# Two projected map tiles and four accumulator tiles for the preparation of keys and values, in place of one and three

## Chip, cores and metric

The kernel runs on one core of one Trainium2 chip. The metric is the device time of one execution in microseconds (us); lower is better. The times before are the median, lowest and highest of three runs.

## What is computed

The input x is 8 images of 256 channels by 32 x 32 positions. Layer 0 normalises each image in groups, projects it to keys and values (kv_w), pools each projected map to four sizes (32, 16, 11 and 5 on a side, together 1426 positions), adds to each a 3 x 3 depthwise convolution, normalises over the channels, and lets 1024 queries in 8 heads attend to the 1426 keys. Layer 1 is a second attention over 1024 tokens and a gated sum of 8 expert networks. All data are float32. The part that the change touches is this:

```python
kv = jnp.einsum('bchw,oc->bohw', x, kv_w)
k_map, v_map = (kv[:, :C], kv[:, C:])
def pooled(t):
    outs = []
    for i, r in enumerate(POOL_RATIOS):
        ...
        p = jnp.einsum('bchw,ph,qw->bcpq', t, Mh, Mw)
        p = p + _depthwise(p, dconv_w[i], dconv_b[i])
        outs.append(p.reshape(B, C, -1))
    return jnp.concatenate(outs, axis=2)
ks_ = _layernorm(pooled(k_map).transpose(0, 2, 1), norm_w, norm_b)
vs_ = _layernorm(pooled(v_map).transpose(0, 2, 1), norm_w, norm_b)
```

## The kernel before, in words

Layer 0's attention (function `attention`) is a main loop over 8 batches x 2 halves of the heads x 2 halves of the queries x 12 chunks of keys, 384 steps in all. A step multiplies queries by keys into the only score tile `sc`[...], ACT takes the exponential into one of six probability tiles `pt`, and PE multiplies the probabilities of the step before by the values into `pv`. Since there is one score tile, the scores of a step wait for the exponential of the step before. Every second step GpSimd issues a DMA that adds one probability tile to another (`add`), and DVE adds these pairs up over the 12 chunks (`sums`).

Between the steps everything else is laid in: preparation of later batches and layer 1 of earlier ones. Who comes next is decided when the program is built, by the class `Flow`: it carries an estimate of each engine's clock, of when each tile is ready and of when its reader is done. Work comes in generators ("threads") with a rank; each says with `yield pe(...)`, `yield ve(...)` and so on what it needs next, or with `yield until(...)` which condition. `step` resumes the lowest-ranked thread that can run, within credits of PE time for each step (`PACE` 4 for ranks under 5, `PACE1` 2 for the others). `finish` lays in work until a condition holds, for example at the beginning of each third of a batch's keys.[...]

The preparation of a batch b is two chains:

- `prepare(b)`, rank 4, one batch after the other: load the image into `xi` (one tile), statistics, normalise, `pool_levels` (pooled input of the three small sizes into `xl`, one tile; GpSimd and DVE), then `maps`, then `queries`, which project the queries and store them to DRAM. The projections are linear, so the pooled input is projected instead of the projected map being pooled.
- `convolve`, rank 7: the taps of each finished map, 8 for each of the four sizes, all on DVE. Then `keys_and_values`, rank 2: `value_tokens` and `key_tokens` transpose the maps, normalise them over the channels and put the keys back.

`maps` takes the four maps of a batch in the order 2, 3 (values), 0, 1 (keys). Each has three slices of columns: two of 512 (the largest size) and one of 402 (the three small sizes). ACT copies each slice from PSUM into the projected map `p`, and writes the middle tap with the bias into the accumulator `acc`. The lists `todo` and `done` hold projected maps and those whose taps are all issued; `read` counts the maps whose taps of the largest size are issued; `freed` counts half batches (two maps) whose accumulators have been turned into tokens. Before the change there is one tile `pmap` for p, and three tiles for `acc`. A map's first two slices wait until all earlier maps' largest taps are issued, and its third slice until all earlier maps are done.

For batch 0 `first_maps` and `first_taps` do the same in another order, with the taps of the large key maps as matmuls on PE; there the third accumulator tile serves as p of map 3. `todo` is given four empty entries for it and `done` gets its four accumulators at the end of `first_taps`.

The last part, the experts, follows attention with its own tiles. A second, general path behind a test (`layer0_general`) is not executed with this data; the diff changes a tile count in it. `kernel` builds the program[...].

Of the kernel before, what the change touches and what calls it, by code (L numbers as in the profile page):

```python
# [142 lines left out]
def layer0_general(tc, kit, nb, x, t1, consts, consts8, vecs, q_t, kv_t, proj_t, gqk_t):  # L143
    nc = tc.nc
    T = kit.tile
    with ExitStack() as ctx:
# [106 lines left out]
        def prepare_keys(b):  # L253

            xt = xs[b]
            st = T(work, [P, 2, 2, 6], "st")
            mv = T(work, [P, 2, 2], "mv")
            for k in range(2):
                for h in range(2):
                    nc.vector.bn_stats(st[:, k, h, :], xt[:, k, h * 512 : (h + 1) * 512])  # L260
                nc.vector.bn_aggr(mv[:, k, :], st[:, k, :, :].rearrange("p h s -> p (h s)"))
            mean, var = mv[:, :, 0], mv[:, :, 1]
            yield
            gm = T(psum, [P, 512], "sm")
            nc.tensor.matmul(gm[:, 0:2], lhsT=grp, rhs=mean, start=True, stop=True)
            mu = T(work, [P, 2], "mu")
            nc.vector.tensor_copy(mu, gm[:, 0:2])
            dev = T(work, [P, 2], "dev")
            nc.vector.tensor_tensor(dev, mean, mu, ALU.subtract)
            nc.vector.tensor_tensor(dev, dev, dev, ALU.mult)  # L270
            nc.vector.tensor_tensor(dev, dev, var, ALU.add)
            yield
            yield
            gv = T(psum, [P, 512], "sm")
            nc.tensor.matmul(gv[:, 0:2], lhsT=grp, rhs=dev, start=True, stop=True)
            gr = T(work, [P, 2], "gr")
            kit.rstd(gr, gv[:, 0:2], 1e-5)
            yield
            xp = xps[b] = T(work, [P, 2, NK], "xp", bufs=2)
            for k in range(2):  # L280
                nc.vector.tensor_scalar(
                    xp[:, k, 0:HW], xt[:, k, :], mu[:, k : k + 1], gr[:, k : k + 1], ALU.subtract, ALU.mult
                )
            yield
            img = xp[:, :, 0:HW].rearrange("p k (h w) -> p k h w", h=32)

            def level(s):
                n = SIDES[s]
                return xp[:, :, OFFS[s] : OFFS[s] + n * n].rearrange("p k (h w) -> p k h w", h=n)


            t2 = T(work, [P, 2, 32, 16], "pool")
            nc.gpsimd.tensor_tensor(t2, img[:, :, :, 0::2], img[:, :, :, 1::2], ALU.add)
            nc.gpsimd.tensor_tensor(level(1), t2[:, :, 0::2, :], t2[:, :, 1::2, :], ALU.add)
            flat = xp[:, :, OFFS[1] : OFFS[2]]
            nc.gpsimd.tensor_scalar(flat, flat, 0.25, 1.0, ALU.mult, ALU.mult)
            yield

            t3 = T(work, [P, 2, 32, 11], "pool")
            nc.gpsimd.tensor_tensor(t3, img[:, :, :, 0::3], img[:, :, :, 1::3], ALU.add)  # L300
            nc.gpsimd.tensor_tensor(t3[:, :, :, 0:10], t3[:, :, :, 0:10], img[:, :, :, 2::3], ALU.add)
            nc.gpsimd.tensor_tensor(t3[:, :, :, 1:11], t3[:, :, :, 1:11], img[:, :, :, 2::3], ALU.add)
            l3 = level(2)
            nc.gpsimd.tensor_tensor(l3, t3[:, :, 0::3, :], t3[:, :, 1::3, :], ALU.add)
            nc.gpsimd.tensor_tensor(l3[:, :, 0:10, :], l3[:, :, 0:10, :], t3[:, :, 2::3, :], ALU.add)
            nc.gpsimd.tensor_tensor(l3[:, :, 1:11, :], l3[:, :, 1:11, :], t3[:, :, 2::3, :], ALU.add)
            flat = xp[:, :, OFFS[2] : OFFS[3]]
            nc.gpsimd.tensor_tensor(
                flat, flat, con[:, None, K_S11 : K_S11 + 121].to_broadcast([P, 2, 121]), ALU.mult
            )  # L310
            yield

            t5 = T(work, [P, 2, 32, 5], "pool5")
            ends = [(i * 32 // 5, -(-(i + 1) * 32 // 5)) for i in range(5)]
            for i, (a, e) in enumerate(ends):
                nc.vector.tensor_reduce(t5[:, :, :, i], img[:, :, :, a:e], AX.X, ALU.add)
            l5 = level(3)
            for i, (a, e) in enumerate(ends):
                nc.vector.tensor_reduce(
                    l5[:, :, i, :], t5[:, :, a:e, :].rearrange("p k h w -> p k w h"), AX.X, ALU.add  # L320
                )
            flat = xp[:, :, OFFS[3] : NK]
            nc.vector.tensor_tensor(flat, flat, con[:, None, K_S5 : K_S5 + 25].to_broadcast([P, 2, 25]), ALU.mult)
            yield
            acc = ks[b] = T(work, [P, 2, NK], "acc", bufs=3)
            for m in range(2):
                yield from project_and_convolve(b, m, acc)
            yield from kit.layernorm(acc, acc, NK, 1e-5, work, psum, (vec[:, V_NW:], vec[:, V_NB:]))

        def prepare_values(b):  # L330
            acc = vs[b] = T(work, [P, 2, NK], "acc", bufs=3)
            for m in range(2):
                yield from project_and_convolve(b, 2 + m, acc)
            yield from kit.layernorm(acc, acc, NK, 1e-5, work, psum, (vec[:, V_NW:], vec[:, V_NB:]))
# [560 lines left out]
def attention(tc, kit, f, outer, ended, nb, consts, x, t1, t2, hn, bounds, vecs, q_t, kv_t, proj_t, gqk_t, wqk, wqkv, vecs1, w1_d, w1c, gate_d, wrc, vecs2, bnvec):  # L895
# [6 lines left out]
    with ExitStack() as ctx:  # L902
# [5 lines left out]
        def T(pool, shape, tag, bufs=1):  # L908
            return f.tile(pool, shape, tag, bufs=bufs)
# [154 lines left out]
        ks, qs, vts = {}, {}, {}  # L1064
        made = [0]
        turn = [-1]
        todo, done, read, freed, key_parts, normalised = [], [], [4], [0], [0], [0]

        def pe(*tiles, tag=None):
            return "PE", tiles, tag  # L1070
# [10 lines left out]
        def until(cond):  # L1081
            return None, cond, None
# [5 lines left out]
        def maps(xp):  # L1088

            for m in (2, 3, 0, 1):  # L1090
                c = m % 2
                yield until(lambda: read[0] >= len(todo) and len(todo) < 3 + 2 * freed[0])
                p = pmap
                acc = T(work, [P, NK], "acc", bufs=3)
                for s0, w in KEY_SLICES:
                    if s0 >= HW:
                        yield until(lambda: len(done) >= len(todo))
                    src = source(xp, s0, w)
                    yield pe(src, tag="sm")
                    ps = small()  # L1100
                    for k in range(2):
                        f.pe.matmul(
                            ps[:, :w],
                            lhsT=kvw[:, k, m * P : (m + 1) * P],
                            rhs=src[:, k, :],
                            start=k == 0,
                            stop=k == 1,
                        )
                    f.act.activation(p[:, s0 : s0 + w], ps[:, :w], AF.Copy)
                    for s, n in enumerate(SIDES):  # L1110
                        a, z = max(OFFS[s], s0), min(OFFS[s] + n * n, s0 + w)
                        if a < z:
                            f.act.activation(
                                acc[:, a:z],
                                ps[:, a - s0 : z - s0],
                                AF.Identity,
                                bias=db(c, s),
                                scale=mid[:, c * 4 + s : c * 4 + s + 1],
                            )
                todo.append((c, p, acc))  # L1120
# [4 lines left out]
            return dy, dx, max(0, -dy), n - max(0, dy), max(0, -dx), n - max(0, dx)  # L1125


        pmap = T(work, [P, NK], "p")
        f.split(pmap, 512, HW)
        first, large, whole, pooled, asked = {}, [], [], [], []  # L1130

        def first_diagonals():
# [11 lines left out]
        def first_maps(xp):  # L1144


            for m in range(4):
                if m < 2:
                    p = T(work, [P, 4, 512], "pt", bufs=6).rearrange("p j q -> p (j q)")
                    acc = T(l1, [P, NK], "v") if m else T(work, [P, NK], "kn", bufs=3)  # L1150
                else:
                    p = T(work, [P, NK], "acc", bufs=3) if m == 3 else pmap
                    acc = T(work, [P, NK], "acc", bufs=3)
                for t in (p, acc):
                    if t is not pmap:
                        f.split(t, 512, HW)
                first[m] = p, acc
            for m, s0 in [(m, s0) for g in (0, 2) for s0 in (0, 512) for m in (g, g + 1)] + [(m, HW) for m in range(4)]:
# [70 lines left out]
        def first_taps():  # L1229
            for m in (2, 3):  # L1230
                yield until(lambda: "maps" in large)
                yield from taps(m - 2, 0, *first[m])
                large.append(("values", m))
            yield until(lambda: whole)
            for m in (2, 3, 0, 1):
                for s in range(1, 4):
                    yield from taps(m % 2, s, *first[m])
                whole.append(m)
            done.extend(first[m][1] for m in (2, 3, 0, 1))
# [1310 lines left out]
```

## Time and profile before

| | |
|---|---|
| three runs, median (lowest to highest) | 3303.81 us (3302.39 to 3315.54) |
| profiled execution, time and span | 3310.0 us, 3308.1 us |
| mean granted clock of TensorE | 0.979 |
| PE, DVE, ACT, POOL busy | 3098.8, 2455.2, 1733.4, 1217.1 us |
| first and last score matmuls of layer 0 | 80.3 and 1953.8 us |
| taps on the accumulators | 928 from p, 32 from an accumulator tile; median 445 ns |
| adds of probabilities by GpSimd's DMAs | 160 of 1024 KB, 32 of 144 KB |

The profile is of one execution. A row of the timeline gives start, length, engine, line of the helper that issued it (all 669 here, so one goes by tile names), operation, output<-inputs and, in brackets, the idle time before it with what ended it. A row of a stretch gives its bounds and length, then busy us and instructions of PE, PEld (weight loads), DVE, ACT and POOL, then the granted clock, the busy share of the DMA engines and GB/s. In the strip of 40 slices each digit is a tenth.

### The profile page before, as it was taken

Reading aid. Unit: us, or ns where it says so; the run is one execution under the profiler, and the core shown is the slowest. Engines: PE = TensorE matmul, PEld = TensorE weight load, DVE = VectorE, ACT = ScalarE, POOL = GpSimd, SP = SyncE. Lnnn points to the kernel's source line nnn. Section 1 sums busy time; section 2 is a strip of 40 time slices with the busy share of each in tenths; the row PEclk is TensorE's granted clock in tenths of the full one; section 3 lists DMA queues with packets and bytes.
Section 4 is the critical chain, followed back from the end, with each engine's and each line's share of the span. In section 5 each row is a group of like instructions: output and inputs, shape, how many; then the busy total and the mean of one; then the engine's idle time right before and its main releaser. Section 6 shows DMA issues by size and latency. Waiting matters only on the chain. (4 is left out here: it accounts for less than half of the span.)

```text
span 3308.1 us, 57168 instructions
## 1 busy us (share of the span) xinstructions
PE 3098.8 (94%) x23038; PEld 1790.7 (54%) x23038; DVE 2455.2 (74%) x4068; ACT 1733.4 (52%) x2330; POOL 1217.1 (37%) x1315
## 2 busy tenths in 40 slices
PE   8687899999999999999899889999999999999997
PEld 4322234334334334334334236767888888888886
DVE  5687688797886887987875455447888787777776
ACT  4476675675676576666666543343333344444442
POOL 2211411412213213213112112007656567777775
PEclk9798999999999999999999999999999999999999
DMA  2357655745646756655556557125434310000000
GB/s 75 84 127 165 131 100 145 147 93 143 142 103 143 147 132 131 132 133 114 125 127 143 122 119 246 60 86 178 153 134 153 139 65 20 20 25 27 20 14 21
DMA packets 110754, 362.70 MB, mean 110 GB/s; under 512 B 13504, under 2 KB 38856, under 8 KB 87248
## 3 DMA queue, kind: packets, MB, share of 16 engines
q0 software_dynamic: 28608, 179.85, 28.2%
q1 hardware_dynamic: 78512, 177.13, 15.5%
q8 instruction: 184, 3.01, 0.4%
q10 hardware_dynamic: 3360, 1.97, 0.2%
q14 instruction: 90, 0.74, 0.1%
HBM read 112.45 MB, written 81.31 MB: 59 GB/s over the span
## 5 line engine op out<-in xcount | busy, mean ns | idle before, releaser
L669 ACT ACTIVATE pt<-sc 128x2048 f32<-128x2048 f32 (+1 forms) x384 | 720.5, 1876 | 298.5 <-PE sc L669 246.5
L669 DVE SCALAR_TENSOR_TENSOR acc<-p,vec,acc 128x225 f32<-128x225 f32 (+7 forms) x928 | 532.7, 580 | 31.3 <-ACT acc L669 6.5
L669 PE MATMUL sc<-q,kn 32*128 32x512 f32 (+1 forms) x3072 | 448.1, 653 | 108.0 <-ACT pt L669 105.8
L669 DVE TENSOR_TENSOR pt<-pt,pt 128x1024 f32<-128x1024 f32 x320 | 384.4, 1244 | 144.3 <-DMA pt<-pt 133.1
L669 POOL DMA_DIRECT2D pt<-pt x192 | 171.4, 894 | 769.3 <-ACT pt L669 592.9
L669 PE MATMUL pv<-pt,vt 128*32 128x512 f32 (+1 forms) x3072 | 420.2, 620 | 0.0
L669 ACT ACTIVATE p1c<-bank 128x256 f32<-128x256 f32 x230 | 87.9, 382 | 565.9 <-PE bank L669 554.3
L669 ACT ACTIVATE h<-h,bnvec 128x512 f32<-128x512 f32 x460 | 348.0, 805 | 63.8 <-DVE h L669 54.7
L669 POOL TENSOR_TENSOR rstd<-rstd,mhalf 128x4 f32<-128x4 f32 (+2 forms) x88 | 108.8, 1237 | 697.7 <-DVE rstd L669 586.3
L669 DVE TENSOR_TENSOR h<-p1c,bank 128x512 f32<-128x512 f32 x230 | 156.7, 681 | 211.6 <-PE bank L669 211.0
L669 PEld LDWEIGHTS sc<-q,kn 32*128 32x128 f32 (+1 forms) x3072 | 116.8, 179 | 320.2 <-ACT pt L669 217.8
L669 POOL TENSOR_TENSOR tm<-h,tm 128x256 f32<-128x256 f32 x210 | 241.8, 1151 | 16.5
L669 DVE TENSOR_TENSOR h<-u,bank 128x256 f32<-128x256 f32 x460 | 234.3, 550 | 7.9
L669 PEld LDWEIGHTS pv<-pt,vt 128*32 128x32 f32 (+1 forms) x3072 | 60.9, 108 | 304.2 <-issue 295.1
L669 POOL TENSOR_TENSOR tm<-h 128x512 f32<-128x512 f32 x105 | 137.9, 1313 | 195.2 <-ACT h L669 194.1
L669 DVE TENSOR_TENSOR h<-h,gate 128x1024 f32<-128x1024 f32 x128 | 203.2, 1588 | 0.5 <-ACT h L669 0.5
L669 PE MATMUL bank<-h,w2e 128*128 128x256 f32 (+1 forms) x604 | 193.3, 448 | 2.8 <-DVE h L669 1.9
L669 PE MATMUL sm<-p,v 128*32 128x256 f32 (+1 forms) x2416 | 192.3, 379 | 0.7 <-ACT p L669 0.7
L669 PE MATMUL y<-t,s3e 128*128 128x256 f32 x768 | 187.0, 379 | 2.2 <-POOL t L669 2.1
L669 PE MATMUL bank<-t,s1e 128*128 128x256 f32 x750 | 183.8, 381 | 3.5 <-DVE h L669 3.5
L669 POOL TENSOR_TENSOR t<-h,t 128x256 f32<-128x256 f32 x216 | 172.9, 800 | 17.0
L669 POOL TENSOR_TENSOR t<-h 128x512 f32<-128x512 f32 x108 | 140.1, 1298 | 105.4 <-DVE h L669 80.0
(315 smaller groups left out, 5448.6 us busy)
## 6 DMA issues: line engine op xcount, KB each, us to landing
pt<-pt POOLq DMA_DIRECT2D x160, 1024.0 KB, 7.5
h<-h SPq DMA_DIRECT2D x118, 512.0 KB, 3.3
xi<-in_x_dram SPq DMA_DIRECT2D x16, 512.0 KB, 6.7
t<-t SPq DMA_DIRECT2D x8, 1024.0 KB, 5.6
res<-t SPq DMA_DIRECT2D x32, 256.0 KB, 4.7
t<-res SPq DMA_DIRECT2D x32, 256.0 KB, 4.6
hn<-res SPq DMA_DIRECT2D x32, 256.0 KB, 4.2
hn<-hn SPq DMA_DIRECT2D x16, 512.0 KB, 4.4
```

Source lines behind the costliest of these rows:

```text
L669: ins = fn(*args, **kwargs)
```

## The change

There are two tiles for p, used in turn, and four for `acc`, in the executed path and in the general one. The conditions are loosened accordingly: a map's first two slices wait until all earlier maps but one have their largest taps issued, its third slice until all earlier maps but one are done. Two maps of batch 1 may be projected before batch 0's accumulators are free; after that two maps for each half batch freed, one more than before in all. `read` begins at 2 and is raised by the two value maps of batch 0. Map 3 of batch 0 has the second tile for its p, no accumulator tile. The room comes from the descriptors of GpSimd's DMAs, which get 4096 bytes of a partition.

```diff
@@ general path: prepare_keys, prepare_values
-            acc = ks[b] = T(work, [P, 2, NK], "acc", bufs=3)
+            acc = ks[b] = T(work, [P, 2, NK], "acc", bufs=4)
...
-            acc = vs[b] = T(work, [P, 2, NK], "acc", bufs=3)
+            acc = vs[b] = T(work, [P, 2, NK], "acc", bufs=4)
@@ attention
-        todo, done, read, freed, key_parts, normalised = [], [], [4], [0], [0], [0]
+        todo, done, read, freed, key_parts, normalised = [], [], [2], [0], [0], [0]
@@ maps
-                yield until(lambda: read[0] >= len(todo) and len(todo) < 3 + 2 * freed[0])
-                p = pmap
-                acc = T(work, [P, NK], "acc", bufs=3)
+                yield until(lambda: read[0] >= len(todo) - 1 and len(todo) < (4 + 2 * max(freed[0], 2) if freed[0] else 6))
+                p = pmaps[len(todo) % 2]
+                acc = T(work, [P, NK], "acc", bufs=4)
                 for s0, w in KEY_SLICES:
                     if s0 >= HW:
-                        yield until(lambda: len(done) >= len(todo))
+                        yield until(lambda: len(done) >= len(todo) - 1)
@@ attention
-        pmap = T(work, [P, NK], "p")
-        f.split(pmap, 512, HW)
+        pmaps = [T(work, [P, NK], f"p{i}") for i in range(2)]
+        for t in pmaps:
+            f.split(t, 512, HW)
@@ first_maps
-                    p = T(work, [P, NK], "acc", bufs=3) if m == 3 else pmap
-                    acc = T(work, [P, NK], "acc", bufs=3)
+                    p = pmaps[m - 2]
+                    acc = T(work, [P, NK], "acc", bufs=4)
                 for t in (p, acc):
-                    if t is not pmap:
+                    if t is not p or m < 2:
                         f.split(t, 512, HW)
@@ first_taps
                 large.append(("values", m))
+                read[0] += 1
@@ kernel
-    nc = _bacc.Bacc("TRN2", target_bir_lowering=False, num_devices=1)
+    nc = _bacc.Bacc("TRN2", target_bir_lowering=False, num_devices=1, dynamic_dma_scratch_size=4096)
```

## The prediction

> **What bounds the kernel now.** I read first the busy shares and the strip of 40 slices on the page, then the busy time of each engine in stretches cut at the batches of the convolution layer's attention, then the same by quarter batch ("unit": one half of the heads, 512 queries, 12 score steps), then the timeline around one hand-over between two maps, and last the DMA and form rows.
>
> ```profile
> PE 3098.8 (94%) x23038; PEld 1790.7 (54%) x23038; DVE 2455.2 (74%) x4068; ACT 1733.4 (52%) x2330; POOL 1217.1 (37%) x1315
> ...
> PE   8687899999999999999899889999999999999997
> ...
> DVE  5687688797886887987875455447888787777776
> ...
> PEclk9798999999999999999999999999999999999999
> ```
>
> TensorE is busy 94%; it is idle 3308.1 - 3098.8 = 209 us. Its low digits, and the low clock, stand in slices 2 to 5 (about 80 to 410 us): the first attention batch and the start of the second. Cut by batch (PE, PEld, DVE, ACT, POOL busy, then clock):
>
> ```profile
> 80.00:325.00 245.00, 184.70 (x1393) 66.97 (x1392) 188.50 (x385) 150.49 (x175) 49.14 (x60) 0.89 0.55 122
> 325.00:562.00 237.00, 217.04 (x2090) 79.04 (x2082) 183.44 (x317) 153.91 (x183) 58.18 (x68) 0.95 0.60 130
> 562.00:811.00 249.00, 234.59 (x2276) 99.58 (x2272) 201.22 (x362) 157.39 (x195) 66.85 (x79) 0.99 0.58 127
> 1041.00:1270.00 229.00, 217.64 (x2224) 83.29 (x2220) 193.71 (x334) 152.42 (x185) 58.07 (x65) 0.99 0.63 137
> 1506.00:1746.00 240.00, 226.12 (x2368) 87.30 (x2360) 190.40 (x339) 155.21 (x191) 57.72 (x71) 0.99 0.57 121
> ```
>
> Length less the first number: PE is idle 60.3 us in batch 0, 20.0 in batch 1, 14.4, (not shown) 9.7, 11.4, (not shown) 9.9, 13.9 and 11.2 in batches 2 to 7: 151 of all 209 us. DVE is idle 35 to 57 us in each of batches 0 to 6. So attention is PE-bound from batch 2 on, with holes; in batches 0 and 1 PE lacks work. By unit:
>
> ```profile
> 325.00:382.00 57.00, 49.98 (x328) 15.68 (x324) 30.10 (x56) 37.98 (x43) 27.77 (x34) 0.86 0.67 132
> ...
> 1041.00:1108.00 67.00, 62.99 (x642) 24.69 (x638) 54.69 (x86) 41.41 (x55) 24.02 (x28) 1.00 0.59 116
> 1108.00:1154.00 46.00, 39.86 (x340) 11.62 (x332) 42.98 (x70) 27.10 (x22) 12.66 (x15) 0.96 0.72 160
> 1154.00:1214.00 60.00, 59.86 (x684) 22.84 (x680) 53.98 (x91) 46.68 (x64) 9.35 (x10) 1.00 0.52 107
> ```
>
> In a steady batch the hole is the second unit: PE idle 6.1 of 46 us while DVE is idle only 3.0; in the unit before, DVE is idle 12.3. DVE lies fallow while preparation is at its load and pooling, then is the limit when the maps' taps come. The hand-over between two maps, on ACT and on DVE:
>
> ```profile
> 1099.20 0.51 ACT L669 ACTIVATE p<-sm 128x402 f32<-128x402 f32 x1 [1.18 <-DVE acc L669]
> ```
>
> ```profile
> 1093.45 5.65 DVE L669 SCALAR_TENSOR_TENSOR acc<-p,vec,acc 128x225 f32<-128x225 f32 x17
> 1101.18 1.76 DVE L669 RECIPROCAL rec<-sx 128x256 f32<-128x256 f32 x1 [2.08 <-ACT sx L669]
> ...
> 1106.37 2.36 DVE L669 TENSOR_TENSOR pt<-pt,pt 128x1024 f32<-128x1024 f32 x2 [1.22 <-DMA pt<-pt]
> 1108.65 3.75 DVE L669 SCALAR_TENSOR_TENSOR acc<-p,vec,acc 128x961 f32<-128x961 f32 x3
> ```
>
> The third slice of the next map cannot go into the one map tile until the last tap of the map before has read it (1099.10); its taps begin at 1108.65, and DVE was idle 3.3 us in between. In the whole run ACT waited 40.3 us, 23 times, for such taps.
>
> [...] the same tap forms, first beside GpSimd's pooling (94 to 104 us), then without it (1094 to 1100 us):
>
> ```profile
> L669 DVE SCALAR_TENSOR_TENSOR acc<-acc,vec,acc 128x20 f32<-128x20 f32 x4 | 2.2, 554 | 0.1
> L669 DVE SCALAR_TENSOR_TENSOR acc<-acc,vec,acc 128x110 f32<-128x110 f32 x4 | 2.0, 490 | 0.1
> ```
>
> ```profile
> L669 DVE SCALAR_TENSOR_TENSOR acc<-p,vec,acc 128x110 f32<-128x110 f32 x4 | 1.3, 334 | 0.1
> L669 DVE SCALAR_TENSOR_TENSOR acc<-p,vec,acc 128x20 f32<-128x20 f32 x4 | 1.0, 242 | 0.1
> ```
>
> [...] the score group that takes 1.14 us took 2.09 at 385.27, and the unit 325 to 382 had clock 0.86. [...] The trace has 28608 packets for GpSimd's 220 DMAs, 130 each or 8.1 per engine[...].
>
> **The change, part by part.** No instruction is added or taken away; the work is issued in another order.
>
> *First start.* Before, the first map of batch 1 waits until batch 0's keys and values are all normalised: its slices run at 160.58 and its taps from 169.10. Its pooled input is ready at 112.3. New: the large slices of two maps may go as soon as both value maps have their large taps (62 us), so from 112 on; the small slice when all first taps end (146.7). A slice takes 1.90, 1.90 and 1.54 us on PE, so taps can start near 150, 19 us earlier, where DVE was idle 7.0 and 4.9 us. Taps of one batch are 74 us of DVE (73.8, 74.4 and 74.9 in three batches) and the four maps ran from 169 to 311, 142 us. DVE was idle 25 us of those; if half of that is recovered, they end at 150 + 142 - 13 = 279, 32 us earlier. Preparation's PE work is 4 x 5.34 (maps) + 4 x 1.90 (queries) + some 13 (48 transposes or so of 0.27) = 42 us. Of it 32/142, or 10 us, crosses from batch 1 into batch 0, into 30 us of PE holes in its last three units: **-10**. The large slices go into the first unit's wait (PE busy 69 of 99 us there), 7.6 us of PE; I count 5, since the bounds on that are 0 and 7.6: **-5**.
>
> *Batch 1.* The next preparation loads its x only after the last query projection; the load was issued at 316.7 and its maps began at 371.7. With batch 1's maps through 32 us earlier, two maps (10.7 us of PE) reach the holes of the first two units (7.0 + 7.5 us): **-8** (bounds 0 and -15).
>
> *Batches 2 to 6.* PE idles 59 us there, 31 of them in the second units. The hand-over bubble goes (3 us of DVE, four maps a batch), and load and pooling of the next batch come to lie beside taps of this one. But PE is the bound: only its holes can be won, and filling a hole earlier is a gain only if that filler is not missed later. I take a third of 31: **-10** (bounds 0 and -31).
>
> *Clock.* Units 2 and 3 of batch 0 and 0 and 1 of batch 1 lose 36 x 0.11 + 39 x 0.05 + 50 x 0.14 + 39 x 0.04 = 14.5 us to the granted clock; fuller units win about half: **-7** (0 to -14).
>
> *Costs.* Pooling (some 27 us of GpSimd a batch) moves beside taps. At 0.24 us more per small tap of 0.5, all of it covered would cost DVE 13 us a batch; DVE's 35 to 57 us of idle hide most. I put 1 us a batch on the path: **+7** (0 to +40). With preparation move 2 loads, the 1 MB copy of x (11.7 us to land), 4 query stores and 2 fetches on SP's queue; behind them stand layer 1's loads (4 to 6 us), whose users sit behind several units of other filler: 0. GpSimd's adds issued in between (0.89 us each) keep their order.
>
> *The ring.* [...] Adds are issued once in two steps (6.3 us at the quickest) and land after
>
> ```profile
> pt<-pt POOLq DMA_DIRECT2D x160, 1024.0 KB, 7.5
> ```
>
> so two are in flight. 0; were only one to fit, 1.2 us each at the quickest pace, some 160 of them less than half exposed: +60 at the very most, which I hold for unlikely. Map 3 of batch 0 now lies in the second map tile instead of an accumulator tile: same instructions, 0.
>
> Sum: -10 - 5 - 8 - 10 - 7 + 7 = -33. The profiled execution took 3310.0 us around a span of 3308.1, so 3277 for it; it lies 6.2 above the median of the runs. Against the median 3303.8 - 33 = **3271**.
>
> **Rivals.** *More than that* (3235): preparation runs ahead by most of a batch, and the two long steps that end batches 1 and 2 (21 and 23 us, keys being finished under a full stop) go too. For it: the bounds above add to -75 without them. Against it: PE was busy in those steps (72.7 of 76 us), so little is lost there. *Filler only changes places* (3298): PE does the same work in attention and what is filled early is missed in later units; only the early start is left, about 6 us. For it: 94% busy, and units 2 and 3 with PE idle 0.1 to 1.1 us. *DVE becomes the bound* (slower): with two maps ready, taps of two follow one another without pause, 37 us of taps in a unit, beside (193 - 74)/4 = 30 us of other DVE work: 67 us against units of 46 to 60. DVE runs in order, so the adds of probabilities (2.36 us a pair) stand behind taps, and the six probability tiles come free late, on which ACT's exponential and then the scores wait. It decides from 1.5 maps in a unit (27 us of taps in 57). At 10 us in one unit of six batches: +60 - 33 = +27, 3331. For it: DVE idle is already 3.0 us in second units. Against it: ACT waited for probability tiles only 24.7 us in the whole run, and DVE has 35 us a batch to spare. *It does not do what it says*: the slices find no PSUM tile or no room in the step, and the order stays; 3304, counted with the second.
>
> **Numbers.** Forecast 0.50 (own range 3250 to 3290); more 0.13; places only 0.21; DVE 0.16. About 0.5% (16.5 us) is what a measurement of this kernel can tell from no change: bounds 3287.3 and 3320.3. Faster: 0.47 + 0.13 + 0.02 = 0.62; same 0.03 + 0.19 = 0.22; slower 0.16. The range 3230 to 3325 leaves out the lower end of "more" and the upper half of "DVE".
>
> **What would show it.** First taps of batch 1 near 150 us; PE idle in the first two batches from 80 towards 55 us, clock there above 0.89 and 0.95; x loads of each batch earlier against its attention; second units with more than 40 us of PE; ACT's wait for taps under 40.3 us; the add still landing in 7.5 us. Wrong it would be if batches 2 to 6 grow, with ACT waiting for probability tiles or GpSimd's adds issuing slower than 0.9 us.

## The result

| | before | after |
|---|---|---|
| median (lowest to highest), 12 runs each on one chip | 3312.31 us (3300.66 to 3317.42) | 3311.52 us (3307.55 to 3318.98) |
| ratio of after to before, 95% interval | | 1.0004 (0.9992 to 1.0017) |
| span of the profiled execution | 3308.1 us | 3310.1 us |
| PE busy and idle in it | 3098.8 and 209.3 us | 3104.6 and 205.5 us |

The change moves the time by nothing that can be measured; 33 us less had been forecast. The page of the kernel after, its busy shares and three strips:

```profile
PE 3104.6 (94%) x22906; PEld 1793.9 (54%) x22906; DVE 2471.6 (75%) x4067; ACT 1735.5 (52%) x2329; POOL 1220.6 (37%) x1309
...
PE   8788879989999989999989889999999999999998
...
DVE  6798989898889869877545545346888887787776
...
PEclk9898989999999999999999999999999999999999
```

DVE's strip is the one that changed: 8s and 9s from slice 2 on, and the low stretch in the middle begins earlier, because the preparation is through earlier (the last tap ends at 1525 us, before at 1719). PE's digits and clock at the start are about as low as they were. Cut by batch (columns as before: length, then PE, PEld, DVE, ACT and POOL busy, then the clock):

```profile
81.00:340.00 259.00, 203.93 (x1485) 75.26 (x1487) 219.44 (x450) 159.12 (x199) 68.26 (x80) 0.89 0.53 119
340.00:575.00 235.00, 203.75 (x1824) 69.84 (x1816) 205.26 (x344) 158.42 (x194) 62.88 (x70) 0.95 0.59 125
...
1530.00:1738.00 208.00, 193.61 (x2028) 75.28 (x2025) 111.06 (x191) 137.07 (x152) 41.83 (x48) 0.99 0.65 135
1942.00:2267.00 325.00, 313.42 (x1254) 219.07 (x1247) 156.30 (x276) 112.08 (x192) 35.45 (x63) 0.97 0.37 129
```

These are batches 0, 1 and 6 and the stretch between attention and the bulk of the experts. The work has moved as foreseen: 22 us of PE work more in batch 0, and batch 6 is 32 us shorter since its preparation is done. But the stretch behind attention grew by 29 us (before 1954 to 2250): it holds the rest of layer 1, of which 24 of 32 units are done when attention ends (25 before). PE idle by stage, length less busy:

| us of PE idle | lead-in | batch 0 | 1 | 2 to 6 | 7 | behind attention | rest | sum |
|---|---|---|---|---|---|---|---|---|
| before | 15.2 | 60.1 | 20.0 | 59.2 | 11.2 | 14.4 | 29.2 | 209.3 |
| after | 14.0 | 55.1 | 31.2 | 57.7 | 13.0 | 11.6 | 22.9 | 205.5 |

Batch 0 wins 5 us and batch 1 loses 11; batches 2 to 6 win 2, the other columns win 8.5 together. PE is idle 3.8 us less in all; with 5.8 us more of PE busy time that gives the span's +2.0.

### The profile page after: what moved, and what is told of

Same layout as the page of the kernel before. It is cut to its first block, busy times and chain, and to the rows that moved or that the text cites. A ratio compares the mean times of both kernels' runs of the same rounds, so it can differ in the third digit from the quotient of the medians.

```text
span 3310.1 us, 56919 instructions
## 1 busy us (share of the span) xinstructions
PE 3104.6 (94%) x22906; PEld 1793.9 (54%) x22906; DVE 2471.6 (75%) x4067; ACT 1735.5 (52%) x2329; POOL 1220.6 (37%) x1309
## 5 line engine op out<-in xcount | busy, mean ns | idle before, releaser
L669 DVE SCALAR_TENSOR_TENSOR acc<-p,vec,acc 128x961 f32<-128x961 f32 (+3 forms) x960 | 570.4, 603 | 29.1 <-ACT acc L669 3.5
L669 PE MATMUL sm<-y,t 128*32 128x256 f32 (+1 forms) x2144 | 179.0, 383 | 1.4 <-ACT p L669 1.4
L669 PE MATMUL sm<-p,v 128*32 128x256 f32 (+1 forms) x2088 | 177.6, 379 | 0.0
```

The source lines that it names most:

```text
L669: ins = fn(*args, **kwargs)
```

## Experiments

Eighteen runs, each with its own runs of the kernel before on the same chip. Three theories were at stake, in the order in which they arose: that PE has the same work and any order gives the same time ("work"); that DVE's queue, filled with taps, takes back what the earlier start brings ("DVE"); and that the new order is only another draw of the plan ("luck").

### The parts of the change

**ring_only**: the kernel before with the smaller room for descriptors.

```diff
-    nc = _bacc.Bacc("TRN2", target_bir_lowering=False, num_devices=1)
+    nc = _bacc.Bacc("TRN2", target_bir_lowering=False, num_devices=1, dynamic_dma_scratch_size=4096)
```

> The kernel before with only the smaller room for GpSimd's DMA descriptors, same order of all work. If the tiles gained time and the ring took it back, this is slower than before by what was gained, some 20 to 40 us, with the 1024 KB adds landing later than 7.5 us or their issue above 0.9 us. If the PE's work is merely moved about (work theory), the ring costs nothing: ratio within 0.998 to 1.002.

Measured: 3305.82 us, 0.9983 (0.9974 to 0.9992). The room costs nothing; an add takes 893 ns to issue (894 before).

**early_only**: the change with both its tiles, but with its looser conditions for the first two maps of batch 1 alone (len(todo) 4 and 5; the third may go one freed half batch earlier than before).

```diff
-                yield until(lambda: read[0] >= len(todo) - 1 and len(todo) < (4 + 2 * max(freed[0], 2) if freed[0] else 6))
+                yield until(lambda: read[0] >= len(todo) - (len(todo) < 6) and len(todo) < (3 + 2 * max(freed[0], 2) if freed[0] else 6))
...
-                        yield until(lambda: len(done) >= len(todo) - 1)
+                        yield until(lambda: len(done) >= len(todo) - (len(todo) < 6))
```

> The changed kernel with the looser conditions for the first two maps of batch 1 alone; from the third map on the conditions of before. Work theory: the same time as both, ratio 0.996 to 1.004; batch 0 gets longer by about as much as its filler grows. If the early start gains (-23 us were forecast for it with batch 1) and the later pipelining loses that again, this is faster by 0.5 to 1%.

Measured: 3282.48 us, 0.9907 (0.9893 to 0.9921). "Work" missed; this is the gain that the forecast's terms for the start add to.

**steady_only**: the change without its early start.

```diff
-                yield until(lambda: read[0] >= len(todo) - 1 and len(todo) < (4 + 2 * max(freed[0], 2) if freed[0] else 6))
+                yield until(lambda: read[0] >= len(todo) - 1 and len(todo) < (4 + 2 * max(freed[0], 2) if freed[0] else 0))
```

> The changed kernel without the early start: batch 1 has to wait for batch 0's accumulators, from then on two maps may be ahead. Work theory: ratio 0.996 to 1.004. If the two parts cancel, this is slower by as much as the early start alone is faster, 0.5 to 1%.

Measured: 3308.12 us, 0.9993 (0.9985 to 1.0001). So one part alone gives -0.9%, the other nothing, and both together nothing; that the second part alone would cost 0.5 to 1% was missed. Batches 0, 1 and 2 of early_only:

```profile
82.00:324.00 242.00, 188.78 (x1387) 70.00 (x1389) 190.07 (x407) 152.13 (x183) 51.54 (x63) 0.91 0.57 128
324.00:536.00 212.00, 197.52 (x1906) 68.65 (x1898) 176.34 (x298) 149.28 (x174) 54.59 (x63) 0.98 0.65 138
536.00:775.00 239.00, 226.97 (x2384) 89.27 (x2376) 191.10 (x344) 153.47 (x187) 55.03 (x69) 0.99 0.62 133
```

Against the whole change, PE is idle 53.2 and 14.5 us in batches 0 and 1 (55.1 and 31.2), and its clock is 0.91 and 0.98 (0.89 and 0.95), by estimate worth 0.02 x 189 + 0.03 x 198 = some 10 us. Those 19 + 10 us add up to nearly all of the 31 us between the two spans; that they are its cause is tried below. DVE has 366 us of work in the two batches; in the whole change it has 425.

### What fills batch 1 of the whole change

DVE and PE of the kernel after around the largest new hole:

```profile
420.79 1.28 DVE L669 BATCH_NORM_STATS2 st<-xi 128x6 f32<-128x512 f32 x2 [6.69 <-DMA xi<-in_x_dram]
...
426.96 1.29 DVE L669 BATCH_NORM_STATS2 st<-xi 128x6 f32<-128x512 f32 x2 [4.64 <-DMA xi<-in_x_dram]
...
428.41 0.71 DVE L669 BATCH_NORM_STATS2 st<-sx 128x6 f32<-128x256 f32 x2
```

```profile
420.18 1.06 PE L669 MATMUL pv<-pt,vt 128*32 128x512 f32 x8
429.17 0.59 PE L669 MATMUL sx<-mv,con 128*128 128x2 f32 x2 [7.93 <-DVE st L669]
```

The image of batch 3 is loaded 144 us earlier than before (406 against 550), into batch 1. DVE keeps to the order of its queue here: it waits 6.69 and 4.64 us for the image's two halves, and behind them stand statistics of layer 1 (428.41) whose input `sx` PE had written by 415.17. PE waits 7.93 us for them, with the next scores behind that. In attention DVE waits 11.3 us for images in all; 8.0 in the kernel before, 0.7 in early_only. Two repairs, and a pair of kernels with less for DVE to do, take this apart.

**after_late_stats**: from batch 2 on the plan takes the image to be ready 10 us later.

```diff
+            if b > 1:
+                f.ready[f.key(xi)] += 10.0
```

> The changed kernel, in which the order is laid down as if each image from batch 2 on landed 10 us later, so that its statistics stand further back in DVE's queue. In the changed kernel DVE stood 6.7 and 4.6 us before the image of batch 3, with layer 1's statistics queued behind, and PE had a hole of 7.9 us. If that one stall is what costs, 10 to 20 us faster than the changed kernel (ratio to before 0.994 to 0.998). If the loss is spread over the batch, the same as the changed kernel.

Measured: 3298.66 us, 0.9962 (0.9953 to 0.9971); 13 us of the 29. DVE no longer waits for an image in attention, and PE idle in batch 1 is 16.9 us. In batches 2 and 3 it is more than in the whole change, 20.9 and 13.9 us (15.8 and 5.0).

**after_hold**: the load itself waits until attention has come to the second half of the heads two batches earlier.

```diff
-                yield until(lambda: len(asked) == 4)
+                yield until(lambda: len(asked) == 4 and turn[0] >= 2 * b - 3)
```

> The changed kernel with both its tiles and all its conditions, and one condition more: a batch's image is not loaded before attention has come to the second half of the heads two batches earlier, where the kernel with the early start alone loads it (284 and 495 us for batches 2 and 3, against 230 and 406 in the changed kernel). If the loss of the later pipelining (29 us against the early start alone) comes from load and pooling falling too early, beside the taps and while layer 1 has nothing for PE, this is near the early start alone: ratio 0.988 to 0.995. If it comes from two maps following one another without a pause, it stays near 1.000.

Measured: 3303.28 us, 0.9981 (0.9972 to 0.9991), outside the 0.988 to 0.995 expected if the early load were the cause. The condition held the loads back less than was meant: batches 2 and 3 are loaded at 232 and 431 us, not at 284 and 495, in the whole change at 230 and 406; only the later images come 82 to 134 us later than there. PE idle in batch 1 is 17.9 us here, yet less is won than with the first repair: there are more holes in batch 3 and behind attention (14.3 and 18.3 us, in the whole change 5.0 and 11.6).

**before_no_large_taps** and **after_no_large_taps**: the eight taps of the largest size are left out for batches 1 to 7, in both kernels.

```diff
-                    yield from taps(c, s, p, acc)
+                    if s:
+                        yield from taps(c, s, p, acc)
```

> The kernel before, leaving out the eight taps of the largest size on DVE in batches 1 to 7 (about 10 of the 18.5 us of taps of each map, 280 us of DVE work in all); output changed. Preparation can then hardly be late. Work theory: PE has the same work and only some of its holes close, so 10 to 40 us are gained at the most. If late taps hold attention back (the forecast's view), over 50 us.

> The changed kernel, leaving out the eight taps of the largest size on DVE in batches 1 to 7 as in the same run of the kernel before (3280); output changed. If it is DVE, loaded by taps that follow without pause beside pooling, that takes the gain back, the gain shows here: some 30 us under that run, ratio 0.980 to 0.984 to before. If PE's work is merely moved about whatever DVE does, the same as that run, 0.988 to 0.993.

Measured: 3280.26 us, 0.9901 (0.9885 to 0.9917), and 3294.48 us, 0.9949 (0.9929 to 0.9969). Less DVE work helps both, the kernel before more than the one after. The 31 us of the kernel before are within what "work" allowed. If DVE's load were what cancels the change, the one after should have been the faster by some 30 us; it is 14 us slower. These 44 us are more than any nudge below moved a kernel (30 us), so DVE's amount of work is hardly what cancels the change.

### Is PE the bound?

**before_less_pe**: the kernel before with half of layer 1's score matmuls left out (one of two halves of the channels).

```diff
-                            for k in range(2):
+                            for k in range(1):
```

> The kernel before, in which layer 1's score matmuls take the first half of the channels only (output changed): 16 x 4 x 2 x 0.24 us or about 15 us of PE a batch less, 120 us of 3099 in all, everything else kept. If attention is bound by PE's work, nearly all of it is gained: 95 to 120 us, ratio 0.963 to 0.971. If waiting for preparation or DVE sets the length, under 60 us.

Measured: 3292.36 us, 0.9941 (0.9918 to 0.9964). Its page:

```profile
PE 3034.7 (92%) x21608; PEld 1729.0 (52%) x21608; DVE 2464.4 (75%) x4068; ACT 1731.0 (53%) x2330; POOL 1217.7 (37%) x1315
```

PE is busy 64 us less, and not the 120 that I had taken. That isn't because less was left out. The matmuls in question, in the kernel before and in this run:

```profile
L669 PE MATMUL sm<-y,t 128*32 128x256 f32 (+1 forms) x2192 | 177.9, 380 | 0.1
L669 PE MATMUL sx<-y,t 128*32 128x256 f32 (+1 forms) x944 | 64.9, 379 | 0.0
```

```profile
L669 PE MATMUL sm<-y,t 128*32 128x256 f32 (+1 forms) x1052 | 89.4, 379 | 0.0
L669 PE MATMUL sx<-y,t 128*32 128x256 f32 (+1 forms) x552 | 40.9, 380 | 0.8 <-ACT p L669 0.7
```

They took 242.8 us and take 130.3, 112 us less. But the rest of PE's work takes 48 us more: the granted clock was 0.964 in this execution (0.964 to 0.970 in all four) and 0.979 before, which on 3035 us is by estimate some 46 us. PE is also idle 53 us more (262.1 against 209.3), two stops for keys of 30 and 38 us among it, where the kernel before has 21 and 23. So 112 us less work leave a span (3296.8 us) that is 11 us shorter; attention ends 10 us later. "Work" falls: PE at 94% is not a queue of work that any order gets through in the same time. It is one draw of the plan, but no nudge below moved a kernel by the 100 us that are missing.

### The draw of the plan

Every choice of the plan depends on those before it. Two numbers that have nothing to do with the change were nudged, to see how far that alone carries.

```diff
-MARGIN = 1.5
+MARGIN = 2.0
```

```diff
-AHEAD = {"DVE": 4.0, "ACT": 2.0, "POOL": 1.0, "SP": 10.0}
+AHEAD = {"DVE": 5.0, "ACT": 2.0, "POOL": 1.0, "SP": 10.0}
```

The first makes early_margin, after_margin and before_margin, the second early_ahead, after_ahead and before_ahead, from early_only, the change and the kernel before.

> The early start alone, with one number of the planner nudged (MARGIN 2.0 instead of 1.5), which has nothing to do with the change: every later choice of the plan is drawn anew. Theory (the later pipelining itself costs the early gain): 0.987 to 0.994 of before, as without the nudge (0.991). Rival (the 29 us between the two was luck of the plan): anywhere from 0.985 to 1.003, and not reliably better than the change with the same nudge.

> The whole change with the same nudge (MARGIN 2.0). Theory: 0.997 to 1.003, and above the early start with the same nudge by 0.005 or more. Rival (luck): it can as well land at 0.99.

> The early start alone with another number nudged (the planner may issue VectorE work 5.0 instead of 4.0 us ahead). Theory: 0.987 to 0.994. Rival: 0.985 to 1.003.

> The whole change with the same nudge (5.0 us ahead on VectorE). Theory: 0.997 to 1.003, above the early start so nudged by 0.005 or more. Rival: as well 0.99.

> The kernel before with MARGIN 2.0. The early start so nudged gave 0.9996, the change so nudged 1.0076. If the early start's gain and the change's cost hold across draws of the plan, this lies between 1.000 and 1.012 (early under it by about 0.009 is the centre: 1.008). If the nudge hurts only the new orders, 0.997 to 1.003.

> The kernel before with 5.0 us ahead on VectorE. The early start so nudged gave 0.9896, the change so nudged 1.006. If the early start's gain holds, 0.996 to 1.003; if it was luck, under 0.993.

In two further rows of draws the repair of the image's stall was put on the nudged change and, as a control, on the early start (after_ahead_late_stats, early_late_stats, early_ahead_late_stats; its diff is that of after_late_stats).

> The change with 5.0 us ahead on VectorE (1.006) and with the image's statistics planned 10 us later from batch 2 on. If the stall on a late image is part of the cost in any plan: 0.999 to 1.004. If it was particular to one plan: 1.004 to 1.009.

> The early start alone (0.9907) with the image's statistics planned 10 us later from batch 2 on. In the early start VectorE waits for an image only 0.7 us in attention. If the repair's gain in the whole change came from a stall that the later pipelining makes: 0.989 to 0.994. If putting the statistics later helps any order: 0.984 to 0.988.

> The early start with 5.0 us ahead on VectorE (0.9896) and the same repair. If the stall is the later pipelining's: 0.987 to 0.993. If the repair helps any order: 0.983 to 0.987.

Measured, as ratios to the kernel before without a nudge (95% interval):

| draw | before | early start alone | whole change |
|---|---|---|---|
| as it is | 1 | 0.9907 (0.9893 to 0.9921) | 1.0004 (0.9992 to 1.0017) |
| MARGIN 2.0 | 1.0023 (1.0015 to 1.0031) | 0.9996 (0.9985 to 1.0006) | 1.0076 (1.0059 to 1.0093) |
| 5.0 us ahead | 1.0031 (1.0019 to 1.0043) | 0.9896 (0.9880 to 0.9913) | 1.0060 (1.0044 to 1.0077) |
| late statistics | | 1.0060 (1.0037 to 1.0083) | 0.9962 (0.9953 to 0.9971) |
| 5.0 us ahead and late statistics | | 1.0075 (1.0053 to 1.0098) | 1.0022 (1.0014 to 1.0030) |

In the three draws without the repair the early start beats both others: the kernel before by 0.3 to 1.4%, the whole change by 0.8 to 1.6%. That speaks against luck alone. But the size isn't to be had from one draw: a nudge moves a kernel by up to 0.9%. Of the ranges expected, the early start's was missed with MARGIN 2.0, and the whole change lay above its range (to 1.003) with both nudges; the distance of 0.005 or more between the two held in both. And the repair, worth 13 and 12 us in the two draws of the whole change, costs the early start 45 us of span (3279.0 to 3324.0) and 59 us (3272.3 to 3331.5). That was expected by neither side. Why shows in the issues of the images' loads, for batches 2, 3 and 7 (start, length), of early_only, of early_late_stats and of the kernel after:

```profile
283.69 0.84 SPq L669 DMA_DIRECT2D xi<-in_x_dram  x2
...
495.20 0.81 SPq L669 DMA_DIRECT2D xi<-in_x_dram  x2
...
1457.32 2.96 SPq L669 DMA_DIRECT2D xi<-in_x_dram  x2
```

```profile
283.84 0.85 SPq L669 DMA_DIRECT2D xi<-in_x_dram  x2
...
520.57 0.86 SPq L669 DMA_DIRECT2D xi<-in_x_dram  x2
...
1519.75 2.51 SPq L669 DMA_DIRECT2D xi<-in_x_dram  x2
```

```profile
229.84 2.47 SPq L669 DMA_DIRECT2D xi<-in_x_dram  x2
...
406.24 2.71 SPq L669 DMA_DIRECT2D xi<-in_x_dram  x2
...
1264.21 1.61 SPq L669 DMA_DIRECT2D xi<-in_x_dram  x2
```

With the old conditions of the later batches the preparation is a chain that closes on itself: load, statistics, pooling, four maps one after the other, queries, next load. A turn takes (1457.32 - 495.20)/4 = 240.5 us, the length of a batch of attention (237 to 243). Here it has no slack: 10 us put into each turn delay the last load by 62 us, and then the keys aren't ready. ACT in early_late_stats, at the end of batch 3's attention:

```profile
1027.03 1.87 ACT L669 ACTIVATE pt<-sc 18x2048 f32<-18x2048 f32 x1 [1.82 <-PE sc L669]
...
1045.94 0.60 ACT L669 ACTIVATE kn<-sx 128x512 f32<-128x512 f32 x1 [1.26 <-PE sx L669]
1046.43 0.59 ACT L669 ACTIVATE kn<-sm 128x512 f32<-128x512 f32 x1
1047.80 1.88 ACT L669 ACTIVATE pt<-sc 128x2048 f32<-128x2048 f32 x1 [0.77 <-PE sc L669]
```

20.8 us lie between the start of the last exponential of batch 3 and that of the first of batch 4, until keys kn of batch 4 are put down. There are five such stops of 20 to 27 us in that run, none above 12.1 us in early_only after the first quarter of batch 0, two (21.2 and 22.7 us) in the kernel before. PE is busy in a stop, with filler that the quarter batch behind it then lacks (22 to 34 us of filler behind a stop in this run, 42 at the start of batch 2, ahead of the first stop): in batches 1 to 6 of 17 kernels here PE idles 8.9 us on average in a quarter batch with under 15 us of filler, 7.4 with 15 to 20, and 1.7 with 30 to 50.

In the whole change a turn is (1264.21 - 406.24)/4 = 214.5 us. The last query projection of batch 7 ends 239 us ahead of its attention instead of 44, and the same 10 us cost nothing.

This fits the 45 us, and not all of the 59. In early_ahead a turn took 222.6 us, with batches of 235, so there was slack; the repair made the turn 249.3 us, more than the 10 us put in. Why is open.

**from_batch_3**: the looser conditions for the first two maps of batch 1 and again from batch 3 on, so that nothing more moves into batches 0 and 1.

```diff
-                yield until(lambda: read[0] >= len(todo) - 1 and len(todo) < (4 + 2 * max(freed[0], 2) if freed[0] else 6))
+                yield until(lambda: read[0] >= len(todo) - (not 6 <= len(todo) < 12) and len(todo) < (3 + (len(todo) >= 12) + 2 * max(freed[0], 2) if freed[0] else 6))
...
-                        yield until(lambda: len(done) >= len(todo) - 1)
+                        yield until(lambda: len(done) >= len(todo) - (not 6 <= len(todo) < 12))
```

> The change with the old conditions for the last two maps of batch 1 and for batch 2; the looser ones for the first two maps of batch 1 and again from batch 3 on. Theory (the cost sits in batches 0 and 1): TensorE idle there under 75 us (86 in the change, 68 with the early start alone), ratio 0.986 to 0.994. Rival (later pipelining costs in every batch): 0.996 to 1.003.

Measured: 3313.95 us, 1.0016 (1.0004 to 1.0028). That the cost can only arise in batches 0 and 1 falls: they are as in early_only (PE idle 67 us), and the holes have gone with the run-ahead, to batches 2 to 5:

```profile
536.00:793.00 257.00, 237.91 (x2444) 90.95 (x2440) 209.74 (x366) 163.33 (x206) 76.49 (x92) 0.98 0.56 120
793.00:1030.00 237.00, 221.48 (x2101) 85.86 (x2096) 202.59 (x369) 154.75 (x190) 63.82 (x71) 0.95 0.60 129
1030.00:1290.00 260.00, 245.68 (x2408) 95.45 (x2408) 229.41 (x407) 169.94 (x218) 64.45 (x75) 0.97 0.57 124
1290.00:1536.00 246.00, 229.46 (x2354) 91.75 (x2346) 217.41 (x377) 157.44 (x194) 61.91 (x72) 0.98 0.58 126
```

PE is idle 19.1, 15.5, 14.3 and 16.5 us in them, 65.5 in all; in early_only 42.0 (12.0, 9.6, 10.0, 10.4). DVE has 859 us of work there against 780, since part of a batch's preparation more falls into them. One of the holes, on DVE and PE of from_batch_3:

```profile
1338.81 8.22 DVE L669 SCALAR_TENSOR_TENSOR acc<-p,vec,acc 128x240 f32<-128x240 f32 x10
1346.95 0.69 DVE L669 TENSOR_TENSOR sm<-sm,rec 128x512 f32<-128x512 f32 x1
1347.67 0.88 DVE L669 SCALAR_TENSOR_TENSOR res<-sm,bv,res 128x256 f32<-128x256 f32 x2
```

```profile
1348.70 3.28 PE L669 MATMUL sm<-y,t 128*32 128x256 f32 x32 [7.33 <-DVE res L669]
1351.90 1.05 PE L669 MATMUL sc<-q,kn 32*18 32x512 f32 x8
```

Ten taps of a map stand ahead of layer 1's vector work; PE's next filler waits 7.33 us for it and the scores stand behind the filler, though nothing holds them: the exponential before them ended at 1340.86. It is the stall at 421 us again with taps in the image's place.

## Why the prediction was wrong

**First start, -10 and -5: right in its times and its direction.** Taps of batch 1 begin at 149 us (150 was forecast), its maps are through at 286 (279). But PE idle in batch 0 fell only from 60.1 to 55.1, a third of the 15 us. In all five kernels with the early start and the old later conditions batches 0 and 1 take 454 to 466 us together, against 474 to 482 in the three kernels before; in the three of the whole change without a repair they take 494 to 514.

**Batch 1, -8, and clock, -7: failed.** They held, or nearly so, while the early start stood alone (PE idle 20.0 to 14.5 us, clock 0.89 and 0.95 to 0.91 and 0.98, and -29 us in time). In the whole change batch 1 has 31.2 us of idle PE and the clock stays at 0.89 and 0.95: the next load, pooling and taps come into the same 235 us. That fuller units win back half of what the clock takes was my estimate, and no run shows it alone: with PE busy 79% of batch 0 the clock is 0.89 in the whole change, with 78% it is 0.91 in early_only. In the costs I put the loads that move along at 0 and looked at SP's queue alone: layer 1's loads stand behind them there, with users "behind several units of other filler". I left out the image's own users, statistics that stand in DVE's queue ahead of layer 1's. That is one term put at nothing, 13 us by its repair.

**Batches 2 to 6, -10: failed.** PE idle went from 59.2 to 57.7 us. The hand-over bubble did go for the most part (the kernel after, ACT in attention):

```profile
ACT p L669 <- DVE acc L669: 10.4, 5, 3.8
```

40.3 us before. It wasn't what made the holes. I took it that PE is the bound and only its holes can be won; before_less_pe shows PE isn't alone in it, and the control with the repair shows what else is: under the old conditions the preparation's turn is about as long as a batch (223 to 246 us, a batch 235 to 240, in the six kernels without a repair). The change does take that away: its preparation ends 239 us ahead. In the holes that were looked at, the order on DVE and PE is what counts: a PE instruction that waits for a vector step behind an image (7.93 us, the kernel after) or taps (7.33 us, from_batch_3) holds back scores that are ready.

**Pooling beside taps, +7: right in kind.** The taps in attention took 545 us, 530 before: +15 us of DVE, of which no run shows how much is on the path. The trace shows which taps lost it: those during which GpSimd computes took, in all, 36 us longer than the median of the same form without it (before: 19), the others no longer. A small tap lost 0.21 to 0.36 us so, where 0.24 was taken. **The ring (the room for descriptors), 0: right**; the adds of 1024 KB land in 7.7 us (7.5). How many of them the smaller room holds was not shown.

```profile
pt<-pt POOLq DMA_DIRECT2D x160, 1024.0 KB, 7.7
```

**The rivals.** "More than that" (its bounds come to -78, not -75, with the large slices' 7.6) saw rightly that the two long steps would go, the longest after the first quarter of batch 0 being 14.8 us now; as was said against it, that gained little. "Filler only changes places" comes nearest by its time (3298), but its reason, that PE has the same work and so the same time, fell with before_less_pe. "DVE becomes the bound" had the right place, vector work behind taps, and not the right measure: DVE is 87% busy in batch 1, and leaving taps out did not bring the change below the kernel before likewise cut. But the wait that it names, ACT's for probability tiles, did grow (attention of the kernel before, then of the one after):

```profile
ACT pt L669 <- DMA pt<-pt: 24.7, 9, 4.4
ACT pt L669 <- DVE pt L669: 6.3, 3, 3.1
```

```profile
ACT pt L669 <- DMA pt<-pt: 41.4, 13, 5.1
ACT pt L669 <- DVE pt L669: 12.1, 4, 4.8
```

That is 31.0 and 53.5 us. In the three draws without the repair the sum is 30 to 35 us in the kernel before, 23 to 48 with the early start alone and 46 to 61 in the whole change. The slower time that the rival drew from it didn't come: batches 2 to 6 take 1163 us together, 1183 before.

**Left open.** Of the 29 us between early_only and the whole change, 13 go with the image's stall (12 in the second draw). A repair is a new draw too, so its size is no surer than that; that the stall and 14 us of idle PE in batch 1 go with it is measured. The rest goes with PE holes and a lower granted clock in batches 0 and 1 (0.89 and 0.95, in early_only 0.91 and 0.98); a queue of taps ahead of a waiting PE is seen in it, and ACT's longer wait for probability tiles. No run takes only these away, and with nudges of up to 0.9% a remainder of 16 us can't be told from the draw.

**A version that beats both**: early_ahead, 3274.88 us, 0.9896 of the kernel before. By the table it is a draw worth keeping as it stands, and not a setting to rely on.

## What to carry to other kernels

Where an order is planned when the program is built, test a change of its conditions under two or three harmless nudges before believing 1%: here one nudge moved a kernel by 0.9%. Before counting on slack won on a preparing chain, ask what the stops cost that it avoids: here more of it, without stops, won nothing. Look for the queue on which the prepared work stands ahead of what the busiest engine waits for: in the kernel after it was DVE's, with 7.93 us of PE in one hole. Before calling an engine the bound because it is 94% busy, take some of its work away, and look at its clock too: 112 us less gave 11, since the rest took 48 us longer at a lower clock (0.964 against 0.979) and PE was idle 53 us more.

## What the runs showed of the hardware

With 4096 bytes for descriptors GpSimd's adds were neither issued nor landed noticeably slower: 893 ns an issue in ring_only and 902 in the kernel after, 894 before; those of 1024 KB landed in 7.7 us in the kernel after, 7.5 before. The kernel before with that alone even ran 0.17% faster (0.9983, 0.9974 to 0.9992); the cause was not looked for.

With 112 us of matmuls left out, the rest of the same kernel's matmuls took 48 us longer, at a mean granted clock of 0.964 against 0.979, and PE was idle 53 us more: the span was 11 us shorter.

In attention of the kernel after, a tap of 16 to 110 elements during which GpSimd computed took 481 to 600 ns on average, without it 234 to 334; one of 961 or 992 elements 1280 and 1320 ns, without it 1215 and 1251. Those during which GpSimd did no more than issue a DMA took within 5 ns of the rest (321 against 322 ns for 100 elements, 1219 against 1214 for 961).
